# The first image's polynomial in seven chunks, a running minimum in place of a reduction, and scores with 64 keys per matrix

## The chip, the cores and the metric

The kernel runs on one core of a Trainium2 chip. The metric is the device time of the program in microseconds. Before the change it was 5033.5 us, the median of 3 runs (5032.83 to 5038.3).

## The reference

32 images x of 64 channels and 56 x 56 pixels go through two layers, all in 32-bit floats. N is 3136, the number of pixels.

```
# layer 0: within each of 8 groups of 8 channels, all products of two and of three channels
y  = x + (W2 @ p2 + b2) * beta2 + 0.1 * (W3 @ p3 + b3) * beta3      # per group
# layer 1: attention of every pixel to every pixel, two softmaxes one after the other
g  = clip(bn1(w_inside @ y), 0, 6)                # values, 64 channels
f  = theta.T @ theta,  theta = y[:32]             # N x N scores
f  = softmax(f, axis=1)                           # over the keys' axis: row by row of the tile
f  = softmax(f, axis=2)                           # over the other axis
out = (f @ g) / H * W
out = bn2(depthwise_3x3(out)) + y
```

The scores are symmetric, so a row of a tile of 128 keys can serve for the first softmax, and the second one's sums come out of the matrix product with a column of ones beside g.

## The kernel before

**Pairs and steps.** Images are worked on in 16 pairs. A pair has 49 steps (`IT`): 24 tiles of 128 keys of its first image, one tile that holds the last 64 keys of both, and 24 tiles of the second. The main loop (line 819) goes over the steps `t`. In a step PE makes the scores of tile t in two halves (`scores`, lines 477 to 504): each half fills a tile `ps` of four PSUM banks with four matmuls, one per bank, each with 128 keys as its stationary matrix (32 rows of theta by 128 columns) and 392 columns of theta as the moving one. Theta stands four times in SBUF, on four blocks of 32 partitions (`th`, written by `load_theta`, line 434), so that the four matmuls stand on different rows of the array. A 32-bit matmul shows as two records in the trace. The tile of the last keys (`kind == 2`) uses two matrices of 64 keys per bank, one per image.

**From scores to weights.** DVE copies a half to the tile `e` in SBUF and keeps its maximum (`tensor_scalar` with `accum_out`, line 501; in the trace TENSOR_SCALAR_CACHE_REDUCE and a DVE_READ_ACCUMULATOR). After the second half, `first_softmax` (line 506) reduces the two maxima to the negated maximum `nm` and ACT computes exp(e + nm) with its sum `z`. `second_softmax` (line 511), one step later, takes the reciprocal `rz` and ACT computes exp(e * rz). Three steps (`LAG`) after its scores, a tile goes into the products with g (`attend`, line 524; tiles `av` and `ax`).

There is one buffer of `ps`, so the scores of a half wait until DVE has read the half before; four buffers of `e`.

**The polynomial.** For each image pair the products of channels are made by POOL from x (`products`, line 303), chunk by chunk of 242 pixels (`PCS`, 13 chunks), and PE multiplies them by the weights (`poly`, `poly_out`), in small units put between the parts of a step. Every chunk loads shifted copies of x: `x0`, `xa`, `x2`, `x4`, `xb` (two DMAs each) and `xc`, by DMAs that SP issues (`load_next`, line 267); `credit` limits how many are issued per half step. A DMA takes one of eight semaphores in turn and waits until the load that had it before has landed.

**The first image.** Before the loop the polynomial of the first image is made by DVE (`ks` counts halves of 32 channels in a pair: `ONE` = (0, 1) is the first image, `TWO` = (2, 3) the second) (`feed(0, c, ONE, dve)`, lines 691 to 724) with the same chunks, buffers and weights; its loads go alternately to SP's and ACT's queues. The values g of the first image follow chunk by chunk (`first_g`). Then `load_theta(0)` copies theta, four DMAs, and the loop begins. The second image's chunks are fed at step 0, for POOL.

**Order.** Every instruction is pinned behind the one before it on its engine (`pin`, line 90), DMA issues among them: the order on each queue is that of the program's text. All recorded lines are that of the helper `call` (L109), so the trace is read by tile names: `ps` scores, `e` weights, `av` and `ax` accumulators, `p` and `q` products, `th` theta, `pp` and `pq` the first image's sums.

Of the kernel before, what the change touches and what calls it, by code (L numbers as in the profile page):

```python
# [11 lines left out]
ALU = mybir.AluOpType  # L12
AX = mybir.AxisListType
PSUM = bass.MemoryType.PSUM
# [56 lines left out]
def tile_poly_conv_attention(  # L71
# [122 lines left out]


    b3row = const.tile([128, C], FP, name="b3row")
    dve.tensor_scalar(b3row, row("beta3_0"), CONV3_SCALE, None, ALU.mult)
# [11 lines left out]
    dve.tensor_tensor(t0, col("b2"), col("beta2_0"), ALU.mult)  # L209
    dve.tensor_tensor(bias0, bias0, t0, ALU.add)  # L210


# [8 lines left out]
    for k in range(GM):  # L221
# [12 lines left out]

    yt = yp.tile([128, 3, N], FP, name="y")
    ys = [yt[:, p, :] for p in range(3)]
    pool.memset(ys[0][C:, :], 0.0)
    prods = {}
    NB = 5
    BLK = [(b * H // NB, (b + 1) * H // NB) for b in range(NB)]  # L240
    stored = set()

    LOADS = {
        "0": [(0, 1, 0, 0)],
        "a": [(0, 1, 0, 1)],
        "2": [(0, 1, 2, 0)],
        "4": [(0, 1, 4, 0)],
        "b": [(0, 2, 5, 0), (1, 2, 1, 0)],  # L250
    }

# [9 lines left out]

    def start(out, in_, queue=sync):
        credit[0] -= 1
        queue.dma_start(out=out, in_=in_)

    def load_next():
        tag, key = plan.pop(0)
        n, c, ks, name, k, queue = key
        p0, w = PCS[c]  # L270
        held[tag] += 1
        ident = f"{n}_{c}_{ks[0]}_{k}"
        if name == "c":
            t = xp.tile([128, 2, PCH], FP, name=f"xc_{ident}", tag=tag, bufs=XB[tag])
            at = slice(ks[0] * 32, ks[-1] * 32 + 32)
            for d in range(2):
                src = bass.AP(
                    x.tensor,
                    ((4 * n + ks[0]) * EXT + 4 * d) * 4 * N + p0,
                    [[EXT * 4 * N, len(ks)], [N, 32], [1, w]],  # L280
                )
                start(t[at, d, :w], src, queue)
            loaded[key[:-1]] = [t[at, d, :w] for d in range(2)]
            return
        t = xp.tile([128, PCH], FP, name=f"x{name}_{ident}", tag=tag, bufs=XB[tag])
        for s0, every, d, grow in LOADS[name]:
            src = bass.AP(
                x.tensor,
                ((4 * n + k) * EXT + d) * 4 * N + p0,
                [[N, 32], [grow * 4 * N, NSLOT // every], [1, w]],  # L290
            )
            start(t[s0::every, :w] if every > 1 else t[:, :w], src, queue)
        loaded[key[:-1]] = t[:, :w]

# [7 lines left out]

    def products(n, c, ks, eng):

# [15 lines left out]
        for k in ks:  # L320
            yield "load", (n, c, ks, "a", k)
            x0[k] = use("0", k)
            xa = use("a", k)
            q = prp.tile([128, PCH], FP, name=f"q_{ident}_{k}", tag="q", bufs=ROOM["q"])[:, :w]
            eng.tensor_tensor(q, x0[k], xa, ALU.mult)
            rounds[0][k] = q
            held["xs"] -= 1
            prefetch()
        for r, of in enumerate(("0", "2", "4", "b")):
            rounds.append({})  # L330
            yield "pr", len(ks)
            for k in ks:
# [3 lines left out]
                p = prp.tile([128, PCH], FP, name=f"p_{ident}_{k}_{r}", tag="pr", bufs=ROOM["pr"])[:, :w]  # L336
                eng.tensor_tensor(p, rounds[0][k], xr, ALU.mult)
                rounds[-1][k] = p
# [6 lines left out]
        p4 = prp.tile([128, PCH], FP, name=f"p4_{ident}", tag="pr", bufs=ROOM["pr"])[at, :w]  # L345
        eng.tensor_tensor(p4, both[0], both[1], ALU.mult)
        rounds.append({k: p4 for k in ks})
# [25 lines left out]

    def feed(n, c, ks, eng):
        todo = [("x0" if name == "0" else "xs", name, k) for k in ks for name in "0a"]
        for name in "24bc":
            todo += [("xc", name, None)] if name == "c" else [("xs", name, k) for k in ks]
        for tag, name, k in todo:

            queue = act if eng is dve and len(plan) % 2 else sync  # L380
            plan.append((tag, (n, c, ks, name, k, queue)))
        feeds.append((products(n, c, ks, eng), None))

# [10 lines left out]

    def poly(n, c, ks, rs, acc=None):

        p0, w = PCS[c]  # L400
        rounds = prods[n, c, ks][0]
        own = acc is not None
        if not own:
            acc = ax[:, AUX:]
        at = slice(ks[0] * 32, ks[-1] * 32 + 32)
        for r in rs:
            for k in ks:
                pe.matmul(
                    out=acc[k * 32 : k * 32 + 32, :w],
                    lhsT=wq[:, r, k % 2, :] if r < NRND else w4[at, k * 32 : k * 32 + 32],  # L410
                    rhs=rounds[r][k],
                    start=own and r == 0,
                    stop=(r == NRND),
                    skip_group_check=True,
                )
            taken["pr" if r else "q"] -= 1 if r == NRND else len(ks)

    def poly_out(n, c, ks, acc=None):

        if acc is None:  # L420
            acc = ax[:, AUX:]
        p0, w = PCS[c]
# [4 lines left out]
        dve.scalar_tensor_tensor(  # L427
            ys[n % 3][at, p0 : p0 + w], acc[at, :w], bias0[at], xc, ALU.add, ALU.add
        )
# [3 lines left out]

    def load_theta(b):
        y = ys[b // 2 % 3]
        p0 = (b % 2) * C
        th = thp.tile([128, N], FP, name=f"th_{b}", tag=f"th{b % 2}")
        for r in range(4):
            start(th[r * 32 : r * 32 + 32, :], y[p0 : p0 + CRED, :])
        ths[b] = th  # L440

# [35 lines left out]
    def scores(t, half):  # L477
        n, kind, q = tile_at(t)
        if half == 0:
            es[t] = ep.tile([128, N], FP, name=f"e_{t}", tag="e")  # L480
            mx = sp.tile([128, 2], FP, name=f"mx_{t}", tag="mx")
            nm = sp.tile([128, 1], FP, name=f"nm_{t}", tag="nm")
            z = sp.tile([128, 1], FP, name=f"z_{t}", tag="z")
            rz = sp.tile([128, 1], FP, name=f"rz_{t}", tag="rz")
            stats[t] = mx, nm, z, rz
        p = ps.tile([128, HALF, BANK], FP, name=f"ps_{t}_{half}", tag="ps")
        for j in range(HALF):
            r = j * 32
            c = half * HALF + j
            for i in (0, 1) if kind == 2 else (kind,):  # L490
                th = ths[2 * n + i][r : r + CRED, :]
                o0, k0, m = (i * C, NQ * QT, TAIL) if kind == 2 else (0, q * QT, QT)
                pe.matmul(
                    out=p[o0 : o0 + m, j, :CH],
                    lhsT=th[:, k0 : k0 + m],
                    rhs=th[:, bass.ts(c, CH)],
                    start=True,
                    stop=True,
                )
        e = es[t][:, half * HALF * CH : (half + 1) * HALF * CH]  # L500
        dve.tensor_scalar(
            e.rearrange("p (j c) -> p j c", c=CH), p[:, :, :CH], 1.0, None, ALU.mult, ALU.max,
            accum_out=stats[t][0][:, half : half + 1],
        )

    def first_softmax(t):
        mx, nm, z, _ = stats[t]
        dve.tensor_reduce(nm, mx, AX.X, ALU.max, negate=True)
        act.activation(es[t], es[t], AF.Exp, bias=nm, scale=1.0, accum_out=z)

    def second_softmax(t):
        _, _, z, rz = stats.pop(t)
        dve.reciprocal(rz, z)
# [175 lines left out]


    put(-1, "aux0", lambda: [feed(0, c, ONE, dve) for c in range(NPC)])
    put(-1, "aux0", lambda: prepare(FOR_G))
    banks = {}

    def bank(c):
        k, r = divmod(c, HALF + NK)
        if r == 0:
            t = ps.tile([128, HALF, BANK], FP, name=f"pp_{k}", tag="ps")
            banks.update({k * (HALF + NK) + i: t[:, i, :] for i in range(HALF)})
        if r >= HALF:  # L700
            banks[c] = pa.tile([128, BANK], FP, name=f"pq_{c}", tag=f"av{r - HALF}")
        return banks[c]

    def first_poly(c):
        acc = bank(c)
        for r in range(NRND + 1):
            advance()
            poly(0, c, ONE, [r], acc)
        advance()
        poly_out(0, c, ONE, acc)  # L710

    def first_g(c):
        for qs in GS:
            if ready(qs) == c:
                g_in(0, qs, 0)
                g_out(0, qs, 0)
                prepare(FOR_G if qs[0] < NQ else FOR_POLY)

    for c in range(NPC):
        put(-1, "aux0", lambda c=c: first_poly(c))  # L720
        if c:
            put(-1, "aux0", lambda c=c: first_g(c - 1))
    put(-1, "aux0", lambda: load_theta(0))
    put(-1, "aux0", lambda: first_g(NPC - 1))


# [4 lines left out]
    for n in range(NP):  # L731
# [43 lines left out]
        for what, hs in zip(todo, at):  # L775
            if what[0] == "p":
                poly_unit(*what[1:], hs)
            else:
                assert what[3] == 1 and hs >= 2 * (base + LAG) or hs > 2 * (base + NQ + LAG) + 1
                assert what[3] == 0 or hs < 2 * (base + NQ + LAG)  # L780
                g_unit(*what[1:], hs)
        if n == 0:
            put(0, "feed", lambda: [feed(0, c, TWO, pool) for c in range(NPC)])
        if n + 1 < NP:
            put(
                max(base - 8, 1), "feed",
                lambda n=n: [feed(n + 1, c, ALL, pool) for c in range(NPC)],
            )
# [26 lines left out]
    place_units()  # L815
    run(-1, "aux0")
    credit[0] = 0
# [118 lines left out]
```

## Time and profile before

| | |
|---|---|
| profiled execution, time | 5033.6 us |
| its span | 5031.8 us |
| mean granted TensorE clock | 0.983 |
| PE busy | 4753.8 us, 94% |
| ACT busy | 4545.5 us, 90% |
| DVE busy | 4222.6 us, 84% |
| POOL busy | 3194.2 us, 63% |
| DMA | 684 MB, mean 136 GB/s |

In a line of the timeline, the first number is the start in us from the start of the span, the second the duration; then come engine, line, operation, output and inputs by the program's names, shapes and a count; in brackets stands the idle time before it and what ended it. PEld is PE's weight load, which overlaps PE. `32*128` is the number of rows and columns of the array that a matmul uses.

### The profile page before, as it was taken

Reading aid. Unit: us, or ns where it says so; the run is one execution under the profiler, and the core shown is the slowest. Engines: PE = TensorE matmul, PEld = TensorE weight load, DVE = VectorE, ACT = ScalarE, POOL = GpSimd, SP = SyncE. Lnnn points to the kernel's source line nnn. Section 1 sums busy time; section 2 is a strip of 40 time slices with the busy share of each in tenths; the row PEclk is TensorE's granted clock in tenths of the full one; section 3 lists DMA queues with packets and bytes.
Section 4 is the critical chain, followed back from the end, with each engine's and each line's share of the span. In section 5 each row is a group of like instructions: output and inputs, shape, how many; then the busy total and the mean of one; then the engine's idle time right before and its main releaser. Section 6 shows DMA issues by size and latency. Waiting matters only on the chain.

```text
span 5031.8 us, 240733 instructions
## 1 busy us (share of the span) xinstructions
PE 4753.8 (94%) x105924; PEld 3340.6 (66%) x105924; DVE 4222.6 (84%) x6962; ACT 4545.5 (90%) x2356; POOL 3194.2 (63%) x4325
## 2 busy tenths in 40 slices
PE   3898999999999999999999999999999999999995
PEld 1465676776767677676766767676676767667663
DVE  4465698898989889898988989898898989889887
ACT  0577899999999999999999999999999999999995
POOL 0667585876858587585857758586775858677000
PEclk7899999999999999999999999999999999999998
DMA  5555656555565555655565565556556555654201
GB/s 144 140 153 152 150 147 149 145 146 143 143 147 144 147 142 144 145 147 139 152 149 137 142 148 148 139 149 149 143 137 145 151 142 145 151 139 120 44 10 33
DMA packets 892956, 684.17 MB, mean 136 GB/s; under 512 B 291584, under 2 KB 877568, under 8 KB 887808
## 3 DMA queue, kind: packets, MB, share of 16 engines
q1 hardware_dynamic: 879368, 659.52, 51.4%
q8 instruction: 828, 13.57, 1.1%
q10 hardware_dynamic: 12536, 9.25, 0.7%
q14 instruction: 224, 1.84, 0.1%
HBM read 565.65 MB, written 25.69 MB: 118 GB/s over the span
## 4 chain that ended last, share of the span: by engine, by line
PE 71%; DVE 21%; DMA 4%; issue 2%; POOL 1%; SPq 1%; ACT 0%; ACTq 0%; POOLq 0%; DVEq 0%
PE av L109 30%; PE ps L109 24%; PE ax L109 16%; DVE e L109 15%; DVE y L109 3%; DMA xc_None<-in_x_dram 2%; DVE num L109 1%; DMA xa<-in_x_dram 1%; SPq L109 1%; POOL p L109 1%; DMA x<-in_x_dram 1%; DVE rd L109 0%; DVE nm L109 0%; POOL q L109 0%; DMA xb<-in_x_dram 0%
## 5 line engine op out<-in xcount | busy, mean ns | idle before, releaser
L109 DVE TENSOR_SCALAR_CACHE_REDUCE e<-ps 128x1568 f32<-128x1568 f32 x1568 | 2806.6, 1790 | 508.1 <-PE ps L109 462.9
L109 PEld LDWEIGHTS av<-gq,e 128*64 128x64 f32 x64512 | 2014.1, 138 | 864.7 <-issue 806.7
L109 ACT ACTIVATE e<-e,nm 128x3136 f32<-128x3136 f32 x784 | 2282.8, 2912 | 310.8 <-DVE rz L109 228.3
L109 POOL TENSOR_TENSOR p<-q,x 128x242 f32<-128x242 f32 (+1 forms) x2418 | 1781.1, 769 | 939.6 <-PE ax L109 843.0
L109 ACT ACTIVATE e<-e,rz 128x3136 f32<-128x3136 f32 x784 | 2270.3, 2896 | 0.0
L109 PE MATMUL av<-gq,e 128*64 128x65 f32 x64512 | 2227.2, 225 | 3.9 <-ACT e L109 3.2
L109 PE MATMUL ps<-th 32*128 32x392 f32 (+1 forms) x12800 | 1489.4, 541 | 109.7 <-DVE e L109 96.7
L109 PEld LDWEIGHTS ps<-th 32*128 32x128 f32 (+1 forms) x12800 | 491.3, 181 | 448.0 <-DVE e L109 368.4
L109 DVE SCALAR_TENSOR_TENSOR y<-tt,wdt,y 128x605 f32<-128x605 f32 (+4 forms) x720 | 742.4, 1032 | 6.7 <-DMA tt<-tr 5.3
L109 POOL TENSOR_TENSOR p<-q,xb 128x242 f32<-128x242 f32 x806 | 592.5, 762 | 230.6 <-PE ax L109 218.1
L109 POOL TENSOR_TENSOR q<-x,xa 128x242 f32<-128x242 f32 x806 | 561.5, 722 | 216.0 <-DMA xa<-in_x_dram 208.2
L109 PE MATMUL ax<-gq,e 128*64 128x65 f32 x12288 | 489.7, 222 | 0.0
L109 PE MATMUL ax<-p,wq 128*32 128x242 f32 (+1 forms) x6448 | 481.5, 373 | 1.5
L109 PEld LDWEIGHTS ax<-gq,e 128*64 128x64 f32 x12288 | 425.3, 138 | 0.0
L109 POOL TENSOR_SCALAR y<-y,bias 128x616 f32<-128x616 f32 (+1 forms) x80 | 162.8, 2036 | 147.5 <-PE ax L109 137.7
L109 PEld LDWEIGHTS ax<-p,wq 128*32 128x32 f32 x6448 | 178.9, 109 | 111.4 <-POOL p L109 18.8
L109 DVE SCALAR_TENSOR_TENSOR y<-ax,bias,xc_None 128x242 f32<-128x242 f32 (+3 forms) x208 | 97.1, 467 | 108.8 <-PE ax L109 103.1
L109 POOL TENSOR_TENSOR p<-xc_None 128x242 f32<-128x242 f32 (+3 forms) x208 | 127.6, 614 | 78.8 <-DMA xc_None<-in_x_dram 68.6
L109 PE MATMUL ax<-wit,y 128*64 128x64 f32 x3136 | 143.8, 223 | 18.6 <-DVE ax L109 9.6
L109 PE MATMUL ax<-p,w 128*32 128x242 f32 (+1 forms) x1612 | 123.9, 369 | 31.6 <-POOL p L109 31.6
L109 ACT ACTIVATION_READ_ACCUMULATOR e<-e,nm 128x1 f32 x784 | 145.6, 186 | 0.0
L109 DVE TENSOR_REDUCE nm<-mx 128x1 f32<-128x2 f32 x784 | 121.7, 155 | 27.2
(73 smaller groups left out, 1368.1 us busy)
## 6 DMA issues: line engine op xcount, KB each, us to landing
x<-in_x_dram SPq DMA_DIRECT2D x2268, 121.0 KB
xb<-in_x_dram SPq DMA_DIRECT2D x1512, 60.5 KB
xa<-in_x_dram SPq DMA_DIRECT2D x756, 121.0 KB
th<-y SPq DMA_DIRECT2D x128, 392.0 KB
xc_None<-in_x_dram SPq DMA_DIRECT2D x360, 121.0 KB
x<-in_x_dram SPq DMA_DIRECT2D x190, 116.0 KB
out_dram<-y SPq DMA_DIRECT2D x64, 308.0 KB
tt<-tr SPq DMA_DIRECT2D x128, 100.0 KB
```

Of the source, the lines that this page charges most:

```text
L109: i = f(*args, **kw)
```

## The change

1. **First image.** Its polynomial gets code of its own ahead of the loop: seven chunks of 448 pixels (`FCS`) in place of 13 of 242, with the four `e` buffers as 28 places for loads and the tiles of y not yet used and `tt` as 21 places for products. Loads of chunks 0 and 1 are issued ahead of the weights' preparation on DVE and ahead of the square roots on ACT; DVE makes the products of chunk 0 ahead of, and of chunk 1 between, the parts of that preparation. xc becomes four loads of 32 rows. Theta is copied in two parts: the first five chunks' columns at chunk 5, the rest at the end. The second image's feed moves from step 0 to chunk 5, with a credit of 12 loads, ahead of the rest of theta on SP.
2. **Running minimum.** DVE's copy of a half is negated, with a minimum in place of the maximum; the second half takes the first half's minimum as a per-partition operand, so its result is the minimum over both. The reduction `nm<-mx` goes away; the first exponential reads exp(-e + nm).
3. **Scores.** Every key tile uses two matrices of 64 keys per bank, on the two halves of the array's columns: eight matmuls per half.

```diff
+    FW = N // 7
+    FCS = [(p, FW) for p in range(0, N, FW)]
+    firsts = [ep.tile([128, N], FP, name=f"first_{i}", tag="e") for i in range(4)]
+    fx, fp = parts(firsts), parts(ys[1:] + [tt])
+    def first_loads(c):
+        def load(dst, k, d, grow, steps):
...
+            (act if fat["q"] % 2 else sync).dma_start(out=dst, in_=src)
+            fat["q"] += 1
+        for name, k in [(a, k) for k in (0, 1) for a in "0a"] + [(a, k) for a in "24b" for k in (0, 1)]:
+            t = fx[fat["x"] % len(fx)]
...
+            for s0, every, d, grow in LOADS[name]:
+                load(t[s0::every, :] if every > 1 else t, k, d, grow, NSLOT // every)
+        for d in (0, 1):
...
+            for k in (0, 1):
+                load(t[k * 32 : k * 32 + 32, :], k, 4 * d, 0, 1)
+    def first_products(c):
+        q = {k: product(xs["0", k], xs["a", k]) for k in (0, 1)}
+        frs[c] = [q] + [{k: product(q[k], xs[a, k]) for k in (0, 1)} for a in "024b"]
+        dve.tensor_tensor(xs["c", 1], xs["c", 0], xs["c", 1], ALU.mult)
+    first_loads(0)
+    first_loads(1)
+    first_products(0)
     b3row = const.tile([128, C], FP, name="b3row")
...
     dve.tensor_tensor(bias0, bias0, t0, ALU.add)
+    first_products(1)
+    first_loads(2)
     s1 = rsqrt_eps("bn1", row("var1"), C)
...
         p = ps.tile([128, HALF, BANK], FP, name=f"ps_{t}_{half}", tag="ps")
...
-            for i in (0, 1) if kind == 2 else (kind,):
-                th = ths[2 * n + i][r : r + CRED, :]
-                o0, k0, m = (i * C, NQ * QT, TAIL) if kind == 2 else (0, q * QT, QT)
+            for i in (0, 1):
+                th = ths[2 * n + (i if kind == 2 else kind)][r : r + CRED, :]
+                k0 = NQ * QT if kind == 2 else q * QT + i * TAIL
                 pe.matmul(
-                    out=p[o0 : o0 + m, j, :CH],
-                    lhsT=th[:, k0 : k0 + m],
+                    out=p[i * TAIL : i * TAIL + TAIL, j, :CH],
+                    lhsT=th[:, k0 : k0 + TAIL],
                     rhs=th[:, bass.ts(c, CH)],
...
         dve.tensor_scalar(
-            e.rearrange("p (j c) -> p j c", c=CH), p[:, :, :CH], 1.0, None, ALU.mult, ALU.max,
-            accum_out=stats[t][0][:, half : half + 1],
+            e.rearrange("p (j c) -> p j c", c=CH),
+            p[:, :, :CH],
+            -1.0,
+            nm[:, :1] if half else None,
+            ALU.mult,
+            ALU.min,
+            accum_out=nm[:, half : half + 1],
         )
     def first_softmax(t):
-        dve.tensor_reduce(nm, mx, AX.X, ALU.max, negate=True)
-        act.activation(es[t], es[t], AF.Exp, bias=nm, scale=1.0, accum_out=z)
+        act.activation(es[t], es[t], AF.Exp, bias=nm[:, 1:], scale=-1.0, accum_out=z)
...
+    prepare(FOR_G)
+    first_poly(0)
+    for c in range(1, NF):
+        first_poly(c)
+        first_out(c - 1)
+        if c + 2 < NF:
+            first_loads(c + 2)
+        if c + 1 < NF:
+            first_products(c + 1)
+        if c == 5:
+            load_theta(0, 0, FCS[5][0])
+            for b in range(NPC):
+                feed(0, b, TWO)
+            credit[0] = 12
+            advance()
+        first_g(c - 1)
+    first_out(NF - 1)
+    load_theta(0, FCS[5][0], N)
+    first_g(NF - 1)
...
-        if n == 0:
-            put(0, "feed", lambda: [feed(0, c, TWO, pool) for c in range(NPC)])
```

`first_poly` multiplies a chunk's products by the weights into a bank of its own, `first_out` adds the bias and x on DVE.

## The prediction

> **What bounds the kernel now.** I read the page's chain first, then busy time by stretch, then the timeline inside each stretch.
>
> ```profile
> PE 71%; DVE 21%; DMA 4%; issue 2%; POOL 1%; SPq 1%; ACT 0%; ACTq 0%; POOLq 0%; DVEq 0%
> ```
> ```profile
> 20.00:139.00 119.00, 57.18 (x410) 25.37 (x408) 60.90 (x173) 1.28 (x1) 0.00 (x0) 0.71 0.55 147
> ...
> 147.00:557.00 410.00, 366.11 (x6738) 231.13 (x6740) 226.84 (x395) 281.09 (x146) 293.56 (x443) 0.94 0.57 151
> 557.00:4690.00 4133.00, 4062.34 (x92694) 2888.63 (x92690) 3651.62 (x5925) 3977.52 (x2058) 2887.62 (x3869) 1.00 0.57 144
> ```
> Columns: stretch, length, busy us of PE, PE weight loads, DVE, ACT, POOL, granted clock, DMA share, GB/s. There are four stages. The first image's polynomial and values run to 139 us with every engine half idle. The first pair (147 to 557) has 49 steps of 8.26 us; there the chain goes through loads called xc and POOL's products. The next fourteen pairs take 4133 us, 686 steps of 6.02 us, with PE busy 98%. The last pair runs 49 steps of 5.80 us. A step is one tile of 128 keys, in two halves of four score banks.
>
> The opening ends so:
> ```profile
> 134.76 0.45 DVE L109 SCALAR_TENSOR_TENSOR y<-pq,bias,xc_None 64x232 f32<-64x232 f32 x1 [2.13 <-PE pq L109]
> ...
> 146.92 1.79 DVE L109 TENSOR_SCALAR_CACHE_REDUCE e<-ps 128x1568 f32<-128x1568 f32 x1 [8.42 <-PE ps L109]
> ```
> I call 146.92 the start E0: the first eviction, delayed by the theta copies, which land one by one to 145.
>
> A half whose bound is the loop of PE and DVE looks like this (late in the last pair):
> ```profile
> 4903.31 1.79 DVE L109 TENSOR_SCALAR_CACHE_REDUCE e<-ps 128x1568 f32<-128x1568 f32 x1 [0.30 <-PE ps L109]
> ...
> 4905.02 0.08 DVE L109 DVE_READ_ACCUMULATOR e<-ps 128x1 f32 x1
> 4905.14 0.15 DVE L109 TENSOR_REDUCE nm<-mx 128x1 f32<-128x2 f32 x1
> ...
> 4905.16 0.94 PE L109 MATMUL ps<-th 32*128 32x392 f32 x8 [0.26 <-DVE e L109]
> 4905.21 0.15 DVE L109 RECIPROCAL rz<-z 128x1 f32<-128x1 f32 x1
> 4905.39 2.91 ACT L109 ACTIVATE e<-e,nm 128x3136 f32<-128x3136 f32 x1
> ...
> 4906.17 1.79 DVE L109 TENSOR_SCALAR_CACHE_REDUCE e<-ps 128x1568 f32<-128x1568 f32 x1 [0.80 <-PE ps L109]
> ```
> There is one score buffer, so the scores start 0.14 us after the accumulator read, and the next eviction 1.01 us after the scores: 2.86 us per half. By its own lines ACT takes 2.91 us for the first and 2.81 for the second exponential, 5.72 a step, and starts 0.1 us after nm: it is not ahead of the loop. Where PE has more to do, PE sets the half (2.91, 3.00, 3.12, 3.14 us) and the accumulator was read 0.18 to 0.39 us before the scores. Counting the halves of the fourteen pairs by that gap (0.15 us or less is the loop): 1065 bound by PE (3208 us), 307 by the loop (925 us), 99 of these after a second half.
>
> **The change part by part.**
>
> **Scores with 64 keys.** Per half, four matmuls (8 records) become eight (16 records). The trace has this form already: the tail tile of each pair.
> ```profile
> 329.11 0.23 PEld L109 LDWEIGHTS ps<-th 32*64 32x64 f32 x16 [0.39 <-DVE rz L109]
> 329.95 1.48 PEld L109 LDWEIGHTS av<-gq,e 128*64 128x64 f32 x48 [0.61 <-issue]
> ...
> 335.30 0.23 PEld L109 LDWEIGHTS ps<-th 32*64 32x64 f32 x16 [0.39 <-issue]
> 336.14 1.13 PEld L109 LDWEIGHTS av<-gq,e 128*64 128x64 f32 x36 [0.61 <-issue]
> ...
> 340.89 0.31 PEld L109 LDWEIGHTS ps<-th 32*128 32x128 f32 x8 [0.39 <-issue]
> 341.76 0.37 PEld L109 LDWEIGHTS av<-gq,e 128*64 128x64 f32 x10 [0.56 <-ACT e L109]
> ```
> From the first score weights to the next work: 0.84 us against 0.87 (to the ns 844 to 849 against 871). The eight run side by side, and the second pass starts earlier behind shorter weight loads. I take 25 ns less PE time. But DVE starts later: the tail tiles' second halves (one signal, as the changed kernel's halves have) release the eviction 1023 ns after the first weights, ordinary ones 1010. So the loop grows by 13 ns. The Trainium skill speaks against this part too (TensorE: Matmul & The Clock Gate, "The cost: per-tile semaphore tail"): a completion tail of 4.7 ns for each tile, so +19 ns for four more. I take the row; the rule would cost another 2.4 us in all. Sum: 1065 PE-bound halves by 25 ns, cut where the loop would take over (2.89 us halves gain about 10), is -25.3 us; 307 loop halves by +13 ns are +4.0; the last pair's 92 loop halves +1.2.
>
> **Running minimum.** 784 reductions go (0.155 us each, 121.7 us of DVE; about 0.12 to 0.15 us of its queue each). That lies beside PE in most halves. Where it was on the path is where DVE itself comes late after nm and the next scores wait for it: 94 halves, 11.4 us at most; I take 6, since PE's own bound is close. ACT gets its bias 0.15 us sooner and has no use for it. Against this the second half's eviction now reads a per-partition scalar. No eviction here has one; the nearest row is wdt (128x9, pointer, 0.23 us) beside TENSOR_SCALAR with immediates (0.15): 65 ns is what I take; bounds 0 and 0.15. It is hidden in PE-bound halves (at least 0.10 us of slack in the 3.00 us ones after the other changes) and paid in 99 + 46 loop halves: +6.4 and +3.0 us. A negated copy and scale -1 cost nothing more: the passes are the same. Scores in all: -25.3 + 4.0 + 1.2 - 6 + 6.4 + 3.0 = **-17 us** (bounds -30 to +3).
>
> **First image in seven chunks of 448.** The bytes are the same, 17.7 MB, in 112 DMAs instead of 182. Before, both queues waited for older loads to land (SP 23.6 us on xc, 16.6 on xa): eight DMA semaphores are shared, so eight loads are out at most, and the xc loads need 4 to 6 us. The 147 GB/s came at 0.55 share, 267 GB/s if never idle. With 1.85 times the bytes in each of eight, 147 x 1.85 = 272 reaches that ceiling; I take 250. The ACT queue no longer stands behind the square roots until 16.88 us: x loads follow the weights at 11 us. So 17 MB / 250 = 68 us, to 79, and 2 to land.
>
> DVE per chunk: back-to-back products of 242 take 0.335 us (six in 2.01) and of 64 columns 0.16, so 0.54 for 448; 11 of them 5.9, one output 0.67, values 1.0: 7.6 us. Seven chunks and the 7 us of weight and batch-norm work (11.68 to 19.03, now moved behind the products) are 60 from the first landing at 20: 80. PE: 24 records of 448 columns, 5.0 us warm and 9.6 cold (16 of 242 take 1.80 or 3.44), beside DVE. Loads are thus last by a little. The Trainium skill (DMA: Bandwidth & Descriptors, "Where 436 GB/s comes from") sets the ceiling at 435 GB/s; by it the loads take 39 us, DVE is the bound and E0 is 85. I go by the row.
>
> After the last landing: products 1.1, matmuls 1, output 0.7, two value groups 2.6, scores 1.7, and 4 for loads that wait for a slot to be read: E0 = **92** (bounds 84 to 105). Five sevenths of theta are copied two chunks earlier and cover the first half's 1568 columns; the rest lands under it. If that cover fails, the 6 us of copies return. Gain 55 us.
>
> **Second images' feed.** Twelve loads are issued on SP ahead of theta's rest. In the first pair SP is the pace (14 loads of 0.62 us for a chunk of some 9 us). xc of the first chunk was issued at 150.44, 3.5 us after E0, now about 2.5 before: 6 us less (bounds 0 and 9), since nothing else in that pair gives way.
>
> **Sum:** 5033.6 (profiled execution; span 5031.8) - 55 - 6 - 17 = **4956 us**; the median 5033.5 is 0.1 lower, no difference.
>
> **Rivals.**
> *The loads keep 147 GB/s.* For it: the share never passed 0.8 in any 5 us. Against: the waits name landed loads, not busy engines. E0 is 11 + 116 + 11 = 138, gain 9: 5033.6 - 9 - 6 - 17 = 5002.
> *PE stays cold.* The granted clock of 0.71 speaks for it; 9.6 + 0.9 us a chunk, seven of them from 24 us, plus 6: E0 = 104, gain 43, 4968. Against it: a PE that busy has been granted more (0.87 between 60 and 80 us).
> *Slower: the eviction with a scalar operand.* If it costs 0.22 us or more, the gains are gone: up to 0.10 it is paid in 209 halves (loop and 2.89 us ones), above that in the 377 halves of 3.00 us too, above 0.22 in those of 3.12: 209 x 0.22 + 377 x 0.12 is 91 us, against 78 + 9 already counted. At 0.4 us: 84 + 113 + 25 = 222, less the 87, is +135: 5169. Against: every pointer row here costs under 0.1.
> *No overlap of the two column halves* (the split doesn't do what it says): 0.65 us more in 1536 halves, 6000 us. The tail tiles exclude it, unless one th read twice behaves differently from two.
>
> **How the numbers follow.** Likeliest 4956: 0.63, own range 4940 to 4974. PE cold 0.17. Old load rate, wholly or in part, 0.10 (4985 to 5005). A faster opening, DVE-bound with the full gain on DVE, 0.04 (4930). Slower 0.05 and the serial scores 0.01. The range is 4928 to 4990. 0.2% is 10 us, what a measurement here can tell: faster 0.93, same 0.01, slower 0.06.
>
> **What would show it.** First eviction between 84 and 105 us. Score bursts 0.84 to 0.85 us to the next weights, evictions 1.02 us after them. No nm reductions; second-half evictions near 1.85 us. Steps of pairs 2 to 15 near 6.00 us, of the last pair near 5.85 (slower). First pair about 399 us from first to fiftieth exponential instead of 404.9. A mean step of the middle pairs over 6.05, or an E0 over 110, makes it wrong.

## The result, and the profile after

The changed kernel takes 4964.3 us (median of 4 runs, 4962.8 to 4981.3) where the kernel before, timed beside it, takes 5034.9 (4 runs, 5032.8 to 5038.3): a ratio of 0.987, 95% interval 0.9845 to 0.9889. That is 8 us above the forecast of 4956 and inside its range. The profiled execution took 4963.2 us with a span of 4961.4, so the two profiles differ by 70.4 us of span.

The chain of the page, and busy time by stretch (length, then busy us of PE, weight loads, DVE, ACT and POOL, granted clock, DMA share, GB/s), both of the changed kernel:

```profile
PE 76%; DVE 12%; DMA 3%; issue 3%; ACT 3%; POOL 1%; SPq 1%; ACTq 0%; POOLq 0%; DVEq 0%
```
```profile
20.00:90.00 70.00, 53.15 (x282) 17.09 (x282) 55.31 (x136) 3.02 (x4) 3.47 (x6) 0.91 0.80 236
98.00:504.00 406.00, 360.03 (x7508) 221.98 (x7516) 219.35 (x344) 281.79 (x147) 287.90 (x434) 0.94 0.57 150
504.00:4615.00 4111.00, 4033.08 (x103440) 2783.95 (x103440) 3583.36 (x5236) 3982.92 (x2059) 2905.36 (x3869) 1.00 0.57 145
```

In the opening PE and DVE are busy for three quarters of the time, with a DMA share of 0.80 against 0.55 before. The first pair (406 us) is as long as it was. The fourteen pairs behind it take 4111 us instead of 4133.

The opening in the timeline, from several engines, in order of time:

```profile
12.44 22.25 ACTq L108 DMA_DIRECT2D first<-in_x_dram  x24
...
36.01 0.26 ACT L108 ACTIVATE s_bn<-v_bn 128x64 f32<-128x64 f32 x1
...
36.30 0.55 DVE L108 RECIPROCAL r_bn<-s_bn 128x64 f32<-128x64 f32 x1 [4.64 <-ACT s_bn L108]
...
85.10 2.54 SPq L108 DMA_DIRECT2D x<-in_x_dram  x4
87.69 2.53 SPq L108 DMA_DIRECT2D xb<-in_x_dram  x4
...
89.83 1.79 DVE L108 TENSOR_SCALAR_CACHE_REDUCE e<-ps 128x1568 f32<-128x1568 f32 x1 [1.00 <-PE ps L108]
90.32 2.49 SPq L108 DMA_DIRECT2D th<-y  x4
91.68 4.39 PE L108 MATMUL ps<-th 32*64 32x392 f32 x16 [1.96 <-DVE e L108]
92.86 1.29 SPq L108 DMA_DIRECT2D xc_None<-in_x_dram  x2
...
96.12 1.85 DVE L108 TENSOR_SCALAR_CACHE_REDUCE e<-ps,nm 128x1568 f32<-128x1568 f32 x1 [4.50 <-PE ps L108]
```

Three things are to be read here. E0, the first eviction, is at 89.83 (predicted 92). The second half of the first step then waits: its scores last 4.39 us instead of 0.92, because theta's second part is issued only at 90.32, behind twelve loads of the second images. And DVE stood idle for 4.64 us, up to 36.3: the square root it needs is on ACT's queue, behind 24 DMA issues.

A half whose bound is the loop, late in the last pair:

```profile
4838.45 0.08 DVE L108 DVE_READ_ACCUMULATOR e<-ps,nm 128x1 f32 x1
...
4838.56 2.91 ACT L108 ACTIVATE e<-e,nm 128x3136 f32<-128x3136 f32 x1
4838.58 0.24 PEld L108 LDWEIGHTS ps<-th 32*64 32x64 f32 x16 [0.49 <-DVE e L108]
4838.58 0.92 PE L108 MATMUL ps<-th 32*64 32x392 f32 x16 [0.35 <-DVE e L108]
4839.43 1.62 PE L108 MATMUL av<-gq,e 128*64 128x65 f32 x48
4839.60 1.79 DVE L108 TENSOR_SCALAR_CACHE_REDUCE e<-ps 128x1568 f32<-128x1568 f32 x1 [1.00 <-PE ps L108]
4841.32 0.08 DVE L108 DVE_READ_ACCUMULATOR e<-ps 128x1 f32 x1
...
4841.46 0.92 PE L108 MATMUL ps<-th 32*64 32x392 f32 x16 [0.41 <-DVE e L108]
...
4842.48 1.85 DVE L108 TENSOR_SCALAR_CACHE_REDUCE e<-ps,nm 128x1568 f32<-128x1568 f32 x1 [0.32 <-PE ps L108]
```

The reduction is gone, the next work on PE follows the scores' start after 0.85 us, the eviction after 1.02, and the second half's eviction takes 1.85 us. The two halves are 2.88 and 2.93 us long, a step 5.81 (before: 5.725). The page's groups give the price of the scalar operand, 1847 - 1790 = 57 ns:

```profile
L108 DVE TENSOR_SCALAR_CACHE_REDUCE e<-ps 128x1568 f32<-128x1568 f32 x784 | 1403.4, 1790 | 312.7 <-PE ps L108 295.4
L108 DVE TENSOR_SCALAR_CACHE_REDUCE e<-ps,nm 128x1568 f32<-128x1568 f32 x784 | 1448.3, 1847 | 256.9 <-PE ps L108 251.4
```

Where the 70.4 us went, by the starts of the first exponentials of the 784 steps:

| stage | before | after | difference |
|---|---|---|---|
| start to E0 | 146.92 | 89.83 | -57.1 |
| E0 to the first exponential | 5.63 | 8.19 | +2.6 |
| 1st to 50th exponential (first pair) | 404.9 | 405.8 | +0.9 |
| 50th to 736th (pairs 2 to 15) | 4132.8 | 4110.9 | -21.9 |
| 736th to 784th (last pair) | 278.2 | 282.0 | +3.8 |
| rest | 63.4 | 64.7 | +1.3 |

The last row is scatter: in other traces it lies between 63.1 and 65.0, and for the changed kernel's own end at 63.1 (e7) and at 64.7 (e11).

### The profile page after: what moved, and what is told of

The parts are those of the page before. It is cut to its first block, busy times and chain, and to the rows that moved or that the text cites. A ratio compares the mean times of both kernels' runs of the same rounds, so it can differ in the third digit from the quotient of the medians.

```text
span 4961.4 us, 263901 instructions
## 1 busy us (share of the span) xinstructions
PE 4711.5 (95%) x118068; PEld 3211.9 (65%) x118068; DVE 4136.2 (83%) x6106; ACT 4554.6 (92%) x2356; POOL 3212.2 (65%) x4325
## 4 chain that ended last, share of the span: by engine, by line
PE 76%; DVE 12%; DMA 3%; issue 3%; ACT 3%; POOL 1%; SPq 1%; ACTq 0%; POOLq 0%; DVEq 0%
PE av L108 33%; PE ps L108 25%; PE ax L108 18%; DVE e L108 10%; ACT e L108 3%; DMA xc_None<-in_x_dram 2%; DVE y L108 1%; SPq L108 1%; POOL p L108 1%; DVE num L108 1%; DMA x<-in_x_dram 1%; DMA first<-in_x_dram 1%; POOL q L108 0%; DMA xa<-in_x_dram 0%; ACTq L108 0%
## 5 line engine op out<-in xcount | busy, mean ns | idle before, releaser
L108 POOL TENSOR_TENSOR p<-q,x 128x242 f32<-128x242 f32 (+1 forms) x2418 | 1820.2, 786 | 842.6 <-PE ax L108 834.8
L108 DVE TENSOR_SCALAR_CACHE_REDUCE e<-ps 128x1568 f32<-128x1568 f32 x784 | 1403.4, 1790 | 312.7 <-PE ps L108 295.4
L108 DVE TENSOR_SCALAR_CACHE_REDUCE e<-ps,nm 128x1568 f32<-128x1568 f32 x784 | 1448.3, 1847 | 256.9 <-PE ps L108 251.4
L108 PE MATMUL ps<-th 32*64 32x392 f32 x25088 | 1450.2, 515 | 120.6 <-DVE e L108 110.8
L108 DVE SCALAR_TENSOR_TENSOR y<-tt,wdt,y 128x605 f32<-128x605 f32 (+4 forms) x720 | 726.2, 1009 | 6.7 <-DMA tt<-tr 5.2
L108 POOL TENSOR_TENSOR p<-q,xb 128x242 f32<-128x242 f32 x806 | 574.9, 740 | 218.8 <-PE ax L108 208.5
L108 PEld LDWEIGHTS ps<-th 32*64 32x64 f32 x25088 | 369.9, 130 | 463.1 <-DVE e L108 381.6
L108 POOL TENSOR_SCALAR y<-y,bias 128x616 f32<-128x616 f32 (+1 forms) x80 | 149.1, 1864 | 149.2 <-PE ax L108 149.2
```

What stands on the lines that cost most here:

```text
L108: i = f(*args, **kw)
```

## The experiments

The kernels were timed on more than one chip, each beside the kernel before, so ratios are compared. The stages are those of the table above, each from one profiled execution ("floor" is the median step of the last pair).

| kernel | ratio to before, 95% interval | E0 | to 1st exp. | first pair | pairs 2 to 15 | last pair | floor |
|---|---|---|---|---|---|---|---|
| changed | 0.9867, 0.9845 to 0.9889 | 89.8 | 8.2 | 405.8 | 4110.9 | 282.0 | 5.813 |
| changed, again (e11) | 0.9855, 0.9840 to 0.9869 | 87.7 | 7.3 | 407.8 | 4109.5 | 282.0 | 5.813 |
| e1 scores alone | 0.9978, 0.9969 to 0.9987 | 141.4 | 5.6 | 409.7 | 4123.4 | 279.3 | 5.751 |
| e2 minimum alone | 1.0023, 1.0015 to 1.0032 | 142.0 | 5.5 | 402.2 | 4150.0 | 280.8 | 5.786 |
| e3 opening alone | 0.9892, 0.9878 to 0.9905 | 90.0 | 8.5 | 402.1 | 4133.1 | 278.2 | 5.725 |
| e6 changed, no minimum | 0.9867, 0.9854 to 0.9881 | 87.9 | 7.6 | 407.5 | 4114.5 | 279.3 | 5.751 |
| e4 theta ahead of feed | 0.9865, 0.9852 to 0.9879 | 89.0 | 5.5 | 414.7 | 4109.7 | 282.0 | 5.813 |
| e5 feed on ACT's queue | 0.9876, 0.9861 to 0.9891 | 93.4 | 5.5 | 403.7 | 4112.8 | 282.0 | 5.813 |
| e7 roots early | 0.9849, 0.9835 to 0.9862 | 83.2 | 8.3 | 406.2 | 4110.8 | 282.0 | 5.813 |
| e8 whole tiles at both ends | 0.9847, 0.9833 to 0.9860 | 90.3 | 7.7 | 402.8 | 4109.7 | 280.7 | 5.785 |
| e10 theta on ACT's queue | 0.9863, 0.9849 to 0.9878 | 91.8 | 5.5 | 407.1 | 4110.9 | 282.0 | 5.813 |
| e9 combined | 0.9850, 0.9833 to 0.9866 | 84.9 | 5.6 | 403.2 | 4112.8 | 278.2 | 5.725 |
| e12 combined, eight loads | 0.9834, 0.9821 to 0.9848 | 85.6 | 5.6 | 408.9 | 4110.5 | 278.2 | 5.725 |

**e1: the scores alone.** The kernel before with this edit:

```
-            for i in (0, 1) if kind == 2 else (kind,):
...
-                o0, k0, m = (i * C, NQ * QT, TAIL) if kind == 2 else (0, q * QT, QT)
...
+            for i in (0, 1):
...
+                k0 = NQ * QT if kind == 2 else q * QT + i * TAIL
...
```

> The kernel before with only the scores changed (two matrices of 64 keys for each tile). As the prediction had it: PE-bound halves lose 25 ns, loop halves gain 13 ns, so 5034.9 - 25.3 + 4.0 + 1.2 = about 5015 us; the floor step of the last pair goes from 5.725 to about 5.75 us, the first eviction stays at 147 us. Rival (completion tail of 4.7 ns per tile): loop halves +19 ns, floor step 5.763 us, about 5017 us. Rival (the gain of the middle pairs came from the missing reductions, not from the scores): middle step stays near 6.02 us, total about 5035 us.

Measured: 5017.5 us beside 5028.8, -11.3. The floor step is 5.751, +26 ns, twice the row's 13; the tail rule's 5.763 is 12 ns too high. Pairs 2 to 15 took 4123.4, of which 8.2 us (6.37 and 1.79 in two neighbouring steps) are one stalled DVE instruction (see e2); without it -17.6. The last pair takes 1.1 more, and the first, at 409.7, 5 to 8 more than in traces with 128 keys (see e8): that is why the total falls short of the expected -20. The rival that put the middle's gain on the missing reductions falls.

**e2: the running minimum alone.**

```
...
-            e.rearrange("p (j c) -> p j c", c=CH), p[:, :, :CH], 1.0, None, ALU.mult, ALU.max,
-            accum_out=stats[t][0][:, half : half + 1],
...
+            -1.0,
+            nm[:, :1] if half else None,
+            ALU.mult,
+            ALU.min,
+            accum_out=nm[:, half : half + 1],
...
-        dve.tensor_reduce(nm, mx, AX.X, ALU.max, negate=True)
-        act.activation(es[t], es[t], AF.Exp, bias=nm, scale=1.0, accum_out=z)
...
+        act.activation(es[t], es[t], AF.Exp, bias=nm[:, 1:], scale=-1.0, accum_out=z)
```

> The kernel before with only the running minimum (no reduction, second half's eviction reads a per-partition scalar). As the prediction had it: -6 for the reductions that go, +6.4 and +3.0 for the scalar operand in the loop halves: about 5038 us; floor step of the last pair 5.725 + 0.057 = 5.78 us (57 ns is what the second-half eviction gained in the changed kernel), middle step 6.02 us. Rival (the reductions were on the path more often than counted): middle step below 6.01 us, total below 5028 us.

Measured: 5040.7 beside 5028.8, +11.9 instead of +3, and 21 runs that spread from 5029.5 to 5062.7. The floor step is 5.786, as expected; twelve of the fourteen middle pairs take 295.2 us each, exactly what they took before. The other two take 303.9, each with this in it (timelines of DVE and POOL of e2, in order of time):

```profile
4539.13 2.67 POOL L109 TENSOR_TENSOR q<-x,xa 128x242 f32<-128x242 f32 x4
4539.69 7.39 DVE L109 SCALAR_TENSOR_TENSOR y<-tt,wdt,y 128x616 f32<-128x616 f32 x1
4541.77 4.64 POOL L109 TENSOR_TENSOR p<-q,x 128x242 f32<-128x242 f32 x7
4547.00 1.78 DVE L109 TENSOR_SCALAR_CACHE_REDUCE e<-ps 128x1568 f32<-128x1568 f32 x1
```

One tap of the depthwise convolution, 0.84 us when POOL is at rest, takes 7.39. It begins while a POOL product is under way (the first of the four at 4539.13), POOL makes ten more without a pause, and the tap ends 0.67 us after the last of them. The other one here (7.37 us) and the one in e1 (6.87) end 0.65 us after POOL's last product. Such a stall costs its pair 8.2 to 8.8 us. All three stand in the middle of the 14th or the 15th pair. The other twelve traces have none: in the kernel before, the 572 taps that overlap POOL's products take 0.82 to 1.42 us, the other 148 at most 0.92. With these 17.6 us taken out, e2's pairs 2 to 15 take 4132.4 us (before: 4132.8), and its last pair takes 2.6 more: what was predicted for this part. Whether such stalls also make the spread of the other runs, and so the miss of 9 us, is not shown: of 21 runs one was profiled.

**e3: the opening alone.** The changed kernel with both edits above reversed.

> The changed kernel with scores and maximum put back as they were: only the new first image and the moved feed. By the prediction: -55 and -6, 4974 us. By the trace of the changed kernel: first eviction 57 us earlier, 3.5 us lost again where the first step waits for theta's second part, nothing from the feed's head start: 5034.9 - 57 + 3.5 = 4981 us, 1st to 50th exponential about 405 us.

Measured: 4975.7 beside 5028.8, -53.1 (interval of the ratio: -61 to -48 us); -61 by the prediction and -54 by the trace were expected. That is nearer to the second, but not for its reason alone. E0 is at 90.0; on that chip the kernels with the old opening, e1 and e2, had it at 141.4 and 142.0, so that the opening gives 51 to 52 us here, not 57. The step to the first exponential is 8.5 us instead of 5.5. The first pair takes 402.1 where the old opening, with the same scores, took 402.2 and 404.9: the head start of the feed is worth 0 to 3 us at most.

**e6: all but the minimum.** The changed kernel with e2's edit reversed.

> The changed kernel with only the running minimum undone (largest value of each half, then a reduction). If the parts add as predicted, -3.4 us: 4961 us; floor step of the last pair 5.812 - 0.057 = 5.755 us, middle step the same as the changed kernel's within 0.01 us. Rival (the reduction costs more beside 64-key scores, since DVE is later against PE there): middle step above 6.00 us and total above 4968 us.

Measured: 4961.9, ratio 0.9867, the same as the changed kernel's. The middle step is 5.998 us, within 0.01 of the changed kernel's 5.993 as expected, and the rival falls; the 3.4 us of the total are too few to be seen. Pairs 2 to 15 are 3.6 us longer, the last pair 2.7 shorter. Taking each of the 49 steps at its median over the fourteen pairs, the minimum shortens eight of them (steps 2, 20 to 22 and 26 by 0.08 to 0.25 us) and lengthens thirteen by over 0.02, most of them by 0.06: -15.8 and +11.2 us over the fourteen pairs. By the same count e6 against e3 gives the scores: -22.0 and +2.1.

**e4: theta first.**

```
         if c == 5:
             load_theta(0, 0, FCS[5][0])
...
-            for b in range(NPC):
-                feed(0, b, TWO)
-            credit[0] = 12
-            advance()
...
     load_theta(0, FCS[5][0], N)
+    for b in range(NPC):
+        feed(0, b, TWO)
+    credit[0] = 12
+    advance()
```

> The changed kernel with the twelve early loads of the second images put behind theta's second part on SP. Theory (the twelve loads delay theta, and their head start is worth little): the second half of the first step no longer waits 4.5 us, first eviction to first exponential 5.5 us instead of 8.2, 1st to 50th exponential within 2 us of 405.8: 2 to 4 us below the changed kernel. Rival (the head start is worth what it is early): xc of the first chunk goes from 5.2 us before the first exponential to about 2.4 after it, and the pair takes that 7 us more: about 3 us above the changed kernel.

Timelines of SP and DVE of e4:

```profile
86.11 2.42 SPq L108 DMA_DIRECT2D th<-y  x4
...
92.61 1.85 DVE L108 TENSOR_SCALAR_CACHE_REDUCE e<-ps,nm 128x1568 f32<-128x1568 f32 x1 [1.77 <-PE ps L108]
...
96.35 1.24 SPq L108 DMA_DIRECT2D xc_None<-in_x_dram  x2
```

The wait of the second half is gone (1.77 us instead of 4.50), the first exponential comes 5.5 us after E0. But xc now comes 1.9 us after it instead of 5.2 before, and the first pair takes 414.7 us, 7 to 9 more. The total is level: in this trace the rival holds, as to the mechanism, and a feed that comes later costs what it is late. In e10 it does not: there xc comes 0.8 us ahead of the first exponential instead of 5.2, and the pair takes 407.1, no longer than in the changed kernel.

**e5: the feed on ACT's queue.**

```
-            credit[0] = 12
+            credit[0] = 14
+            early[0] = act
             advance()
+            early[0] = sync
```

`start`, which issues each load, takes its queue from `early[0]`.

> The changed kernel with the first chunk of the second images' feed (14 loads with both xc) on ACT's queue instead of SP's. SP then has theta's second part next: no wait of 4.5 us in the first step, first eviction to first exponential 5.5 us. xc of the first chunk is issued before the first eviction, as the prediction had it. Theory (the first pair is paced by SP's 14 loads a chunk, and chunk 1 starts on SP at about the same distance from the first exponential as in the changed kernel): first pair 404 to 408 us, total 3 to 4 us below the changed kernel. Rival (it is the first chunk's xc that costs the 6 us): first pair 400 us, total about 10 us below.

xc of the first chunk is issued at 80.1 us, 13 before E0, and the first exponential follows E0 by 5.5 us. Still the total is not better (4968.4 beside 5033.2, runs from 4961.9 to 4983.0), and E0 has moved to 93.4. The timelines of DVE and POOL of e5, and then the same places of the changed kernel:

```profile
76.64 7.36 DVE L108 TENSOR_TENSOR y<-tt,first 128x448 f32<-128x448 f32 x7
...
77.24 6.27 POOL L108 TENSOR_TENSOR p<-q,x 128x242 f32<-128x242 f32 x6
```
```profile
77.20 3.82 DVE L108 TENSOR_TENSOR y<-tt,first 128x448 f32<-128x448 f32 x7
...
87.89 3.98 POOL L108 TENSOR_TENSOR p<-q,x 128x242 f32<-128x242 f32 x6
```

The early loads let POOL begin its products while DVE still makes the first image's. Side by side, seven of DVE's take 7.36 us instead of 3.82 and six of POOL's 6.27 instead of 3.98. The difference of 3.5 us is as much as E0 moved (93.4 instead of 89.8). The Trainium skill (SBUF — State Buffer, "SBUF: two separate sides") has the rule: a DVE operation with two inputs in SBUF and a POOL operation that reads SBUF lock a shared port for the whole instruction, and the other waits. Both products are of that kind, and the rows nearly agree: strictly one after the other, at 3.82 and 3.98 us, they would take 7.8. The first pair, with chunk 1's loads 3 us earlier against the first exponential, took 403.7.

**e7: the roots early.** Both additions on DVE and square roots on ACT move from behind the third chunk's loads to ahead of them:

```
     first_loads(1)
+    roots1 = root_in("bn1", row("var1"), C)
+    roots2 = root_in("bn2", col("var2"), 1)
     first_products(0)
...
```

> The changed kernel with the two square roots on ACT ahead of the third chunk's loads, their additions on DVE ahead of the first products. DVE no longer waits 4.6 us for a square root at 36 us. If DVE is the bound of the opening: first eviction at 85 us, total 4.6 us below the changed kernel. If the loads are (DVE then waits for them instead): first eviction at 88 to 90 us, total within 2 us.

Timelines of ACT, DVE and SP of e7, and of SP of the changed kernel:

```profile
28.14 0.26 ACT L108 ACTIVATE s_bn<-v_bn 128x64 f32<-128x64 f32 x1
...
30.55 0.54 DVE L108 RECIPROCAL r_bn<-s_bn 128x64 f32<-128x64 f32 x1
...
70.47 4.00 SPq L108 DMA_DIRECT2D th<-y  x4
...
83.23 1.79 DVE L108 TENSOR_SCALAR_CACHE_REDUCE e<-ps 128x1568 f32<-128x1568 f32 x1 [0.91 <-PE ps L108]
```
```profile
77.06 3.94 SPq L108 DMA_DIRECT2D th<-y  x4
```

No wait before the reciprocal, and E0 at 83.2. Over all kernels with the late roots E0 lies between 87.7 and 91.8 (e5, slowed by POOL, apart), with the early ones (e7, e9, e12) between 83.2 and 85.6. The total is 4956.2 beside 5033.2; its ratio of 0.9849 is below the changed kernel's 0.9867 and 0.9855, with intervals that overlap.

The loads did not come to be the bound in DVE's stead: they came sooner too. SP was through with them 6.6 us earlier (theta's first copy is next on its queue), and they ran at 258 GB/s between 20 and 84 us, 242 in the changed kernel. The two hold each other up. A load needs a place that DVE has read, and in the changed kernel SP issued none for 10.5 us from 31.7 us on, 5.6 of them waiting for a product that DVE had not made; with the early roots this gap is 6.7 to 7.1 us. So a stop of DVE delayed the loads behind it, and the bound of the opening was DVE's chain with its waits.

**e8: whole tiles in the first and the last pair.**

```
-            for i in (0, 1):
+            whole = kind != 2 and (n in (0, NP - 1))
+            for i in (0,) if whole else (0, 1):
...
+                m = QT if whole else TAIL
...
```

> The changed kernel with scores of whole 128-key tiles in the first and the last pair, 64 keys in the fourteen between. Last pair: floor step 5.812 - 0.026 = 5.786 us, -1.2 us. First pair: in the six traces so far it took 402.1 to 404.9 us with 128 keys and 405.8 to 409.7 with 64. If 64 keys are the cause: about 402 us, total 5 to 6 us below the changed kernel. If it is chance from run to run: 402 to 409 us, total about 1 us below.

Measured: ratio 0.9847, floor 5.785, first pair 402.8. That fits the first theory, but e12, which has whole tiles there too, took 408.9. Of the six traces with 128 keys there, five lie at 402.1 to 404.9 and one at 408.9; the six with 64, leaving out e4 and e5 with their changed feeds, lie at 405.8 to 409.7. A cost of 64 keys in the first pair is likely and not settled.

**e11: the changed kernel again.**

> The changed kernel itself once more, beside the others on the same chip, for the scatter of its stages from one execution to another: first eviction at 89 to 91 us, 1st to 50th exponential 403 to 409 us (the five traces with 64 keys and the same feed so far: 405.8 to 409.7), middle step 5.99 us, floor step 5.813 us, ratio to the kernel before 0.986 to 0.988.

All within what was expected. E0 differs by 2.2 us, the first pair by 2.0, the pairs behind it by 1.4: smaller differences than these are not read from single traces.

**e10: theta's second part on ACT's queue.**

```
+    queue[0] = act
     load_theta(0, FCS[5][0], N)
+    queue[0] = sync
```

`start`, which issues each copy, takes its queue from `queue[0]`.

> The changed kernel with theta's second part on ACT's queue, which has nothing to do until the first exponential; the feed's loads stay where they are on SP. Theory (the twelve loads ahead of it on SP are what makes theta late): first eviction to first exponential 5.5 us instead of 8.2, xc of the first chunk issued at about 90.3 instead of 93.0 us, so its lead over the first exponential stays 5 us, first pair 404 to 408 us: 2.7 us below the changed kernel. Rival (the copies themselves take the time, wherever they are issued): first exponential 8 us after the first eviction, no gain.

The first exponential comes 5.5 us after E0, yet nothing is gained (0.9863). Timelines of SP and ACT's queue of e10, and its waits of SP between 74 and 105 us (total, times, longest):

```profile
85.35 0.55 SPq L108 DMA_DIRECT2D x<-in_x_dram  x1
88.35 2.56 ACTq L108 DMA_DIRECT2D th<-y  x4
90.68 0.54 SPq L108 DMA_DIRECT2D xa<-in_x_dram  x1
...
96.42 1.24 SPq L108 DMA_DIRECT2D xc_None<-in_x_dram  x2
```
```profile
SPq L108 <- DMA th<-y: 5.6, 3, 4.8
```

SP stood for 4.8 us in the middle of the twelve loads, until a theta copy that ACT had issued landed. The eight DMA semaphores are shared by both queues, and this load's turn came behind that copy. xc was issued at 96.4 instead of 90.3. e9, with the same edit, shows it too: SP waited 4.4 us.

**e9 and e12: combinations.** e9 takes the early roots, theta on ACT, whole tiles in the first and last pair, and in the last pair the two minima with a reduction. e12 takes the same without ACT's queue, but only eight of the feed's loads ahead of theta on SP:

```
-            credit[0] = 12
+            credit[0] = 8
             advance()
 ...
     load_theta(0, FCS[5][0], N)
+    credit[0] = 4
+    advance()
```

> The changed kernel with four edits together: square roots ahead of the third chunk's loads, theta's second part on ACT's queue, whole 128-key tiles in the first and last pair, in the last pair the smallest value of each half and a reduction instead of the scalar operand. If the parts add: 4964 - 6.6 (first eviction at 83 us) - 2.7 (first exponential 5.5 us after it) - 4 (first pair about 402 us) - 1.2 - 2.7 (floor step of the last pair back at 5.725 us) = about 4947 us, ratio to the kernel before 0.983. If SP, POOL and PE of the first pair give the earlier start back: first pair 408 us and more, total about 4953 us.

> The changed kernel with the square roots ahead of the third chunk's loads, whole 128-key tiles in the first and last pair, no scalar operand in the last pair, and eight instead of twelve loads of the feed ahead of theta's second part on SP (the other four right behind it). Theory (each load ahead of theta costs its 0.64 us of SP while theta is late, and the first pair does not need the lead): first eviction at 83 us, first exponential 5.5 to 6 us after it instead of 8.2, xc of the first chunk still about 2 us ahead of it, first pair 402 to 404 us: 4964 - 6.6 - 2.5 - 4.3 - 1.2 - 2.7 = about 4947 us, ratio 0.983. Rival (the lead counts one for one): first pair 405 us and more, 4950 us or above.

e9: 4955.2 us (4951.1 to 4962.4), 8 above its expectation; its profiled execution took 4951.1, with E0 at 84.9 instead of 83, the first pair 1 us and pairs 2 to 15 some 2 us longer than taken. e12: 4952.4 (4948.4 to 4953.5), ratio 0.9834, the lowest here: by the ratios 11 us below the changed kernel as e11 ran it and 17 below its first runs, though the intervals of e12 and e11 overlap. Timelines of SP and DVE of e12:

```profile
83.33 2.48 SPq L108 DMA_DIRECT2D th<-y  x4
85.60 1.79 DVE L108 TENSOR_SCALAR_CACHE_REDUCE e<-ps 128x1568 f32<-128x1568 f32 x1 [1.11 <-PE ps L108]
...
89.29 1.85 DVE L108 TENSOR_SCALAR_CACHE_REDUCE e<-ps,nm 128x1568 f32<-128x1568 f32 x1 [1.89 <-PE ps L108]
```

Theta's wait is gone without ACT's help. The first pair took 408.9 us, 5 to 7 more than expected. Against e8, xc comes later after the first exponential by 2.4 us at the second chunk, 4.4 at the 11th and 8.2 at the 16th. The rival, that the lead counts, fits this; it does not fit e9, whose lead was smaller still (1.2 us) and whose first pair took 403.2. Nor does it fit the other traces: leave out e4 and e5, and leads between 0.8 and 5.4 us stand in no order with the pair's time, neither with 128 keys nor with 64. What sets the pace there stays open.

## Why the prediction was right, and where not

**The sum.** 78 us were predicted, 70.4 came, in the profiled executions. E0 was 2.1 us better than taken; scores and minimum together -18.1 instead of -17. Missing are 2.6 us at theta, 6.9 in the first pair and 1.3 at the end, the last of them scatter. The gain of 57.1 us up to E0 leans on one trace of the kernel before (146.9). On the chip of e1, e2, e3 and e6 the old opening had E0 at 141.4 and 142.0 and the new one at 90.0 and 87.9: 51 to 54 us, where 55 were predicted.

**E0 (92; measured 89.8, and 87.7 to 91.8 in the others).** The number held, the reason only in part, so that the hit is in part luck. The loads were to be last, at 250 GB/s; they ran at 236 GB/s with a share of 0.80, and e7 shows that DVE's waits held them up. The prediction summed DVE and the loads each for itself and took the longer; here each waited for the other. The bound of 80 us on DVE left out the wait for the square root: the step said that ACT's loads no longer stand behind the roots, and did not turn it round, that the roots now stand behind 24 issues. That wait (4.64 us) and 3.6 us of waits for loads after the first landing make up most of the difference to 89.8. The ceiling of the Trainium skill (DMA: Bandwidth & Descriptors, "Where 436 GB/s comes from"), weighed there, would have said 85 with DVE as the bound. The bound was the right one and the rate was not: in e12, with E0 at 85.6, the loads went at 256 GB/s between 20 and 84 us, not 435. (The same section gives some 358 GB/s where loads from HBM are the limit; by that figure 17 MB are an estimated 47 us, and DVE is the bound as well.)

**"The rest lands under it": the first step that failed.** The first half's columns covered nothing of the second part, since it is issued behind the twelve loads. The step named these loads as ahead of theta and charged nothing for them. With theta ahead of them, behind eight of them or on another queue, the first exponential follows E0 by 5.5 to 5.6 us, with twelve ahead by 7.3 to 8.5: 1.7 to 3 us were lost, not the 6 that were named if the cover failed.

**"xc ... now about 2.5 before: 6 us less": the second.** xc of the first chunk was issued 3.0 us after E0, as before (3.5), because the twelve loads (9 us of SP with their waits) and theta stand ahead of it. Against the first exponential, which is late itself, it was 3.1 us earlier (5.2 us ahead instead of 2.1). Of this the trace keeps 2.9 us at chunk 1 and 3.1 at chunk 2, and nothing at the end of the pair. And e5, where xc was 13 us ahead of E0, did not bring 6 us either. A late feed cost 7 to 9 us for 7 in e4 and nothing for 4.4 in e10. Nor is SP alone the pace of that pair, as the step had it. In the changed kernel's first pair it waited 75 us for POOL to have read a place (total, times, longest, between 98 and 503 us):

```profile
SPq L108 <- POOL p L108: 55.5, 117, 1.9
SPq L108 <- POOL q L108: 19.2, 51, 1.3
```

**Scores (-25.3 + 4.0 in the middle).** By e6 against e3: -22.0 + 2.1. The size of a half is right, 26 ns less where PE is the bound and 13 more in the loop; the tail rule of the Trainium skill (TensorE: Matmul & The Clock Gate, "The cost: per-tile semaphore tail"; +19) would put e1's floor at 5.763, measured 5.751, a difference of 6 ns for each half. In the last pair +1.2 was predicted, +1.1 measured. The first pair was not costed at all; if e8's reading holds, it is 4 us.

**Minimum (-6 + 6.4 in the middle, +3.0 in the last pair).** Two errors that offset each other, which is luck: by steps -15.8 + 11.2, in the last pair +2.7. The gain had been bounded at 11.4, which e2 alone gives (-11.0); behind shorter scores it is larger. The operand costs 57 ns (65 taken), in thirteen or fourteen steps of a pair rather than the seven halves counted.

**Rivals.** The loads at the old 147 GB/s (236 measured), a cold PE (granted clock 0.91 between 20 and 90 us), an operand of 0.22 us or more and serial halves of the scores are all excluded.

## What to carry to other kernels

When a step is moved onto a queue, go down that queue instruction by instruction and ask of each one behind it who waits for it: here loads moved ahead held up theta, and issues moved ahead of a square root held up DVE. Two engines that wait for each other are no two sums of which the longer counts: a stop of one delays the other. Two engines made busy at once may share something: look at what each row costs when the other engine rests. A stage that scatters by 2 us from one execution to the next can't show an effect of 3 us in one trace; several kernels that share the stage can.

## What the runs showed of the hardware

- **DVE and POOL with inputs in SBUF.** Side by side, a DVE product of two SBUF tiles (128x448) took 1.05 us instead of 0.55 (e5). More than that: a DVE tap that met an unbroken row of POOL products waited for ten further ones, 7.39 us instead of 0.84 (e2), and this cost 8.2 to 8.8 us of its pair each time: three times in two of the fourteen traces (e1, e2). That the port is the cause is argued from the ends of the three taps and the rule; no run took POOL's products away.
- **Queues that share semaphores.** A load on SP waited 4.8 us for a copy on ACT's queue (e10), and 4.4 us in e9.
- **A scalar operand per partition** costs an eviction of 128x1568 elements 57 ns, 1847 against 1790.
